# A planned transformer kernel on one core: the division of the exponentials in plain column order, on either of two engines, and a new order of the work

## The chip, the cores and the metric

The kernel runs on one core of a Trainium2 chip. The metric is the device time of one execution in microseconds, the median of the runs. The core has five engines with a queue each: TensorE (PE, with its weight loads PEld), VectorE (DVE), ScalarE (ACT), GpSimd (POOL) and SyncE (SP), which issues most of the transfers here. A queue is worked in order; engines wait for each other by semaphores.

## The reference

There are 32 sequences of 256 tokens with 256 features, all in float32. The output is `x + ffn(cond(x, f))`.

```python
# cond: queries from f, keys and values from x, 16 heads of 16, one extra self column per query
q = (f + b_self) @ Wq + bq;  k = (x + b_prev) @ Wk + bk;  v = x @ Wv + bv
score = concat(mask(q @ k.T * SCALE), sum(q * k_self) * SCALE)
h = (softmax(score) applied to v and v_self) @ Wo + bo
# ffn: two layers of
qkv = shift_token(h) @ wqkv                  # 8 heads of 64
q, k = rotary(l2norm(q) * qs), rotary(l2norm(k) * ks)
h = h + local_attention(q, k, v) @ wo        # windows of 128 that look one window back; softmax
g = layernorm(shift_token(h)) * lg + lb
a, g = split(g @ w1 + b1);  h = h + (a * gelu(g)) @ w2 + b2
```

The change touches the softmax of the local attention: the exponentials of each row are divided by their sum.

## The kernel before

**Groups.** Sixteen groups of two sequences each (`G = 2`) run through the same stages: `prepared` and `conditioned` (the cond layer), `attention` and `feedforward` for each of the two layers, `finished`. Activations of a group lie in one of two kept tiles `stream`, features on the partitions.

**A recorded program and a planner.** The kernel's engine calls do not issue anything. `Plan.record` stores each as a node with a cost (`price`) and its dependences. Everything that PE does between two calls of `plan.unit` is one PE unit, named in the profile by its PSUM tile: `S`, `ST`, `AV` are the cond attention; `q`, `k`, `v`, `qkT`, `sc`, `exT`, `av`, `wout` the local attention; `mean`, `var`, `rs`, `w` the feed-forward; `cq`, `ck`, `cs`, `vals`, `self`, `nmT`, `ohT`, `turn`, `co` the rest of cond. `Plan.run` plays the nodes through a list schedule of its own, with prices for every engine, for hops between engines, for PSUM banks (8) and SBUF slots, and the resulting order is what `Plan.issue` emits (line 567 for every instruction). Which unit PE takes next is chosen by `policy` at the end of `tile_kernel`: the score is the age of a unit (`AGE * u.stand`), a cost for a change of PE's tile mode (`SWITCH`), backlogs of the fed engines (`OVER`, `STAY`, `ENTER`), and `FEED`, `MOST`, `BANKS`. `u.stand` is a place in an ideal order, 215 us per group, shifted unit by unit by the tables `SHIFT`, `FIRST` (first group) and `FINAL` (last two groups). So the tables and the prices set the order of the whole program.

**Tile modes of PE.** A matmul uses the full 128x128 array, or one of the tiled modes: two or four row tiles (`("rows", 2)`: `qkT`, `sc`, `exT`; `("rows", 4)`: `S`, `ST`), two or four column tiles (`("cols", 2)`: `av`; `("cols", 4)`: `AV`). A unit of full matmuls that stands behind one in column tiles can stay in that mode (`tiling`, `parted`): each matmul is then issued in 2 or 4 parts side by side. In the profile `128*64` and `128*32` are the column tiles, `64*128`, `17*128` and `18*128` the row tiles.

**Either engine.** Nodes of engine `X` (`either`) are copies out of PSUM; `put` in `Plan.run` gives each to DVE or ACT, to whichever would end it first by the plan's backlog.

**The softmax of the local attention** (`weights`). For each of two heads (`i`) and two windows (`w`; one or two blocks of 128 keys) DVE adds the mask and takes the row maximum (`ex<-sc,misc`, which frees the PSUM bank of `sc`), ACT takes the exponential with the row sum (`ex<-ex,nm,rq`, `den`), DVE takes the reciprocal of `den` and multiplies the rows by it (`ex<-ex,den`), always on DVE, through a view with the columns in another order: for the wide one `es[:, i, 1:3, :].rearrange("p k q -> p q k")`, so that the inner loop has two elements 128 columns apart. Then PE transposes `ex` (`exT`). There are 1024 of these multiplications, half of 128 columns and half of 256.

**POOL** adds the two parts of the rotated q and k (`raw<-raw,rot`), raises norms to the power -1/2 (`rq`, `ss`), scales k (`raw<-raw,ss`), and does some sums (`at`, `tv`, `sq`, `xs`, `ot`).

Of the kernel before, what the change touches and what calls it, by code (L numbers as in the profile page):

```python
# [22 lines left out]
G = 2  # L23
# [125 lines left out]
class Node:  # L149


    def __init__(self, engine, unit, number):
        self.engine, self.unit, self.number = engine, unit or self, number
        self.ops, self.cost, self.table, self.load = [], 0.0, None, 0.0
        self.after, self.then, self.ready, self.tiles = {}, [], 0.0, set()


class Plan:
# [15 lines left out]
    def __init__(self, tc, engines, pools, make):  # L174
        self.tc, self.engines, self.pools, self.make = tc, engines, pools, make
        self.nodes, self.units, self.unit_, self.group, self.place = [], [], None, 0, 0.0
        self.stage, self.stages, self.done = 0, {}, set()


    def tile(self, pool, name, shape):  # L180
# [52 lines left out]
    def record(self, engine, name, args, kw):  # L233
# [6 lines left out]
        if engine == "PE":  # L240
            node, wide = u, int(np.prod(out.shape[1:]))
            u.soft = u.soft and name == "matmul" and kw["lhsT"].shape[1] == 128
            cost = (2 if name == "transpose" else 4) * (wide + 2) / 2400 / u.streams
            if name == "transpose" and u.streams > 1:
                cost = max(cost, 0.062 / u.streams)
            cost = max(cost, 0.2) if wide < 64 else cost
            u.small += wide < 64
            turn = 0.65 if name == "transpose" else 1.0 if wide >= 64 else 0.0
            u.weight += cost * turn * self.WORK.get(u.kind, 1.0)
            u.place += cost  # L250
            self.place += cost
        else:
            node = self.node(engine, u)
            self.edge(u, node)
            if name == "dma_start":

                dst, src = kw["out"].shape, kw["in_"].shape
                run = min(dst[-1], src[-1])
                cost, node.load = 0.55, int(np.prod(dst)) / run * max(0.048, run * 4 / 24e3) / 16
            else:  # L260
                cost, node.table = self.price(engine, name, args, kw, size)
                if engine == "X":
                    node.either = {"V": cost, "S": 0.068 + size / 1267}
                u.feeds[engine] = u.feeds.get(engine, 0.0) + cost
# [10 lines left out]
    def price(self, engine, name, args, kw, size):  # L275

        if engine in "VX":
            extra = 0.02 if name == "reciprocal" else 0.0
            if name == "scalar_tensor_tensor":
                extra = 0.06  # L280
            return 0.065 + extra + size / 960, "any" if engine == "X" else None
        if engine == "S":
            func = args[2] if name == "activation" else None
            table = "exp" if func is AF.Exp else "gelu" if func is AF.Gelu else "any"
            extra = 0.315 if "accum_out" in kw else 0.11 if table == "gelu" else 0.0
            extra += 0.09 if func is AF.Identity else 0.0
            return 0.068 + size / 1267 + extra, table
        power = any(v is ALU.pow for v in args)
        return (0.35 + 0.158 * size if power else 0.1 + (0.00187 if size <= 256 else 0.00215) * size), None

# [3 lines left out]
    def run(self, policy):  # L294
# [4 lines left out]
        units, self.backlog = [], {e: 0.0 for e in "VSGDX"}  # L299
        left = {n: len(n.after) for n in self.nodes}  # L300
        self.kind, self.table, pe, blocked = ("full", 1), "any", 0.0, 0.0
        self.begin()
        self.tick, self.filled, self.warm = 0, 0.0, False
        for n in self.nodes:
# [3 lines left out]
        for u in self.units:  # L308
            for tiles in u.takes.values():
                for t in tiles:  # L310
                    t.lead = u.cost if t.lead is None else t.lead
                tiles.sort(key=lambda t: t.lead)
        self.idle = self.switches = self.cold = self.wire = 0.0

        def put(n):
            if n.engine == "PE":
# [40 lines left out]
        while todo:  # L357
# [12 lines left out]
            if e != "PE":  # L370
                ready = [n for n in waiting[e] if n.ready <= t]
                n = min(ready, key=lambda n: self.rank(n, e))
                waiting[e].remove(n)
                cost = n.cost
                if e == "S" and n.table not in ("any", None, self.table):
                    self.table, cost = n.table, cost + 1.3
                now[e] = t + cost
# [3 lines left out]
                todo -= 1  # L381
                end = t + cost
                if n.load:
                    self.wire = max(self.wire, end) + n.load
                    end = self.wire + self.LANDING
                ended(n, end)
                continue
            fit = {u: fits(u) for u in units if u.ready <= t}
# [148 lines left out]

    def rank(self, n, e):
        other = e == "S" and n.table not in ("any", None, self.table)
        return n.ready + 2.0 * other, n.number  # L540


    def parted(self, u):
# [8 lines left out]
    def issue(self, order):  # L552
# [7 lines left out]
        for n in order:  # L560
# [3 lines left out]
            for name, args, kw in ops:  # L564
                if n.engine in "VS" and name == "copy":
                    name = "tensor_copy" if n.engine == "V" else "copy"
                ins = getattr(self.engines[n.engine], name)(  # L567
                    *[real(v) for v in args], **{k: real(v) for k, v in kw.items()}
                )
# [3 lines left out]
class Engine:  # L573
# [12 lines left out]


SHIFT = [
    156, 528, 54, -76, 49, 292, -28, 245, 120, -102, -425, 52, -30, 35, 68, 22, 33, 22, -208,
    -4, 119, -41, 61, 69, 90, 152, 19, 32, -62, -238, 52, -2, 49, -168, 13, -85, -54, -65, 36,  # L590
    64, 112, -439, -349, -167, 223, -408, -5, 62, -46, -234, 56, -27, 119, -7, -45, 96, -17,
    -38, 61, -374, -335, -58, 1, -150, -372, -152, -51, -265, -409, 8, 67, -53, 114, -41, -17,
    -83, 34, 68, 48, 60, -261, -99, -7, -76, -335, -100, -105, -191, -306, -58, 15, -102, 32,
    -23, -66, 39, -309, -188, 106, -258, 33, -30, -139, 22, -141, 82, -290, -255, 32, 19, -99,
    134, 126, 14, -15, -222, -574, -156, 97, 93, -32, -241, 50, 152, -118, -41, -45, 21, -102,
    20, 47, 3, 15, 55, 169, -56, -24, 43, 199, -247, 143, -97, -15, -223, -41, -95, -88, -212,
    -127, -29, -32, -285, -545, -142, -265, -8, -118, -6, 152, 84, -122, 25, 14, 4, 18, 141, 60,
    166, -454, -139, 25, -127, -186, -20,
]
FIRST = [  # L600
    0, 0, 0, 0, 0, 0, 0, 0, 10, 35, -9, 213, 102, 95, 210, -345, -65, -122, -290, 49, -201, 6,
    -193, -61, -7, 106, 99, -6, -100, -16, 106, 13, 65, -266, -137, 7, -58, 247, 58, 69, 48, 1,
    -114, -155, -32, -173, -34, 65, 135, 130, -117, 69, 71, 117, 272, 156, 73, -3, -1, -31, -33,
    -133, 51, 151, 175, 239, 445, 215, 231, 120, 135, 97, -3, -90, -188, -357, -32, -64, -276,
    -297, -374, -330, -535, -346, -72, -135, -217, 156, 27, 182, 40, -174, -48, 77, -252, -118,
    -307, -246, 33, -96, -400, -238, -150, -69, -239, 6, 79, 152, 26, -38, -60, -358, -15, -155,
    89, -99, -69, -60, 87, -3, -114, -222, -118, 60, -143, -246, -29, -171, -319, -115, -49,
    -17, -96, -75, -88, 113, 144, -56, -6, 35, -9, -141, -41, -74, -183, -115, -131, -49, -79,
    109, -65, -145, 55, -88, -244, -157, -153, -264, -181, -118, -121, -82, -23, -37, -86, -83,
    -110, -213, -219, -209, -160, -63, 0, 0,  # L610
]
FINAL = [
    0, 0, 0, 0, 0, 0, 0, 0, 56, -34, 24, 16, 12, 140, -55, -63, -14, 1, -33, -84, -66, -53, -46,
    -145, -40, -121, 67, -19, -32, -29, 98, 97, 8, 45, -119, -130, -61, -106, 67, 94, -33, 8,
    54, 33, 8, -94, -222, -47, -210, -95, -90, -11, -121, 156, 49, 10, 43, 87, 7, 64, -144, -81,
    35, -80, 47, -31, -76, -182, 53, 86, 32, 67, 229, 49, 115, 31, 6, -10, -135, 40, 27, -79,
    -83, -8, 108, -110, 63, -40, -249, -98, -95, -18, -170, -139, -28, -12, -41, 76, 83, 116,
    59, -9, 65, -157, -74, -50, -119, -145, -16, -25, 13, 6, 73, -2, -181, -184, -151, -49, -97,
    116, -8, 56, 187, 15, 69, -31, -42, -59, 109, 161, 193, 112, 209, 211, 117, 80, 41, 59, 77,
    -84, 136, 47, 92, -54, 145, 66, 93, 1, -60, 152, -30, 108, 108, -119, 50, -9, -29, -39, 44,  # L620
    -113, -118, -128, -103, 66, 10, -89, -27, -49, -2, -10, 53, 34, -67, -8,
]


# [1 line left out]
def tile_kernel(ctx: ExitStack, tc: tile.TileContext, a: dict, out: bass.AP):  # L626
# [415 lines left out]
    def attention(l, b, res):  # L1042
# [80 lines left out]
        def weights(c, sc):  # L1123
# [29 lines left out]
                        accum_out=den[:, i, w : w + 1],  # L1153
                    )
            vec.reciprocal(den, den)

            for i in range(2):
                for w in range(2):
                    part = (
                        es[:, i, 1:3, :].rearrange("p k q -> p q k")  # L1160
                        if w
                        else es[:, i, 0, :].rearrange("p (k q) -> p q k", k=2)
                    )
                    vec.tensor_scalar(part, part, den[:, i, w : w + 1], None, ALU.mult)
            return es

        def turned(ess):
# [207 lines left out]

    PERIOD = 215.0
    STRETCH, AHEAD, LAST = 2.75, 3, 14
    AGE, SWITCH, OVER, STAY, ENTER = 0.02, 1.5, 1.0, 6.0, 4.0
    HURRY = 0.0
    FEED, MOST, BANKS = 1.0, 3.0, 0.0  # L1380


    numbers = {}
# [68 lines left out]
```

## Time and profile before

| | |
|---|---|
| median of 3 runs | 3427.64 us (3423.55 to 3428.22) |
| the profiled execution | 3422.27 us, of which the span is 3420.5 us |
| mean granted clock of TensorE | 0.990 |
| PE busy | 3348.6 us, 98% of the span |
| DVE, ACT, POOL busy | 2161.9 us (63%), 1780.5 us (52%), 1163.4 us (34%) |
| `ex<-ex,den` on DVE | 1024 instructions, 351.4 us |
| loads of ACT's function table | 96 of 1283 ns |

How to read it: the groups overlap, so PE is occupied from one end to the other except in the first 125 us or so, where loads from memory and a halved clock hold it. From about 800 to 2650 us the groups repeat each other exactly, one every 207.2 us; a stretch of that length is the unit in which a change of the steady part is read. A busy PE can still stand inside a matmul's record, so idle time on PE is only a part of what it loses.

### The profile page before, as it was taken

How to read it: one execution, taken by the hardware profiler on the slowest of the kernel's cores; microseconds unless marked ns; L12 is line 12 of the kernel's file. 1: busy time of each engine (PE TensorE's matmuls, PEld its weight loads, DVE VectorE, ACT ScalarE, POOL GpSimd, SP SyncE). 2: the span in 40 equal slices, each digit the busy share in tenths (PEclk: the TensorE clock that was granted, in tenths of full speed). 3: DMA queues.
4: the chain of work that ended last, by engine and by line, in shares of the span. 5: the costliest groups of instructions: out<-in, count | busy, mean ns of one | idle time of the engine just before them, and what ended most of it. 6: DMA issues, size and time to landing. Idle time of an engine off the chain costs nothing.

```text
span 3420.5 us, 69279 instructions
## 1 busy us (share of the span) xinstructions
PE 3348.6 (98%) x25984; PEld 1908.7 (56%) x25984; DVE 2161.9 (63%) x6673; ACT 1780.5 (52%) x4537; POOL 1163.4 (34%) x1195
## 2 busy tenths in 40 slices
PE   6999999999999999999999999999999999999998
PEld 5665556465564655656455564655646556465554
DVE  3558567485675747657485674847657486574763
ACT  0556456473554726456373563735547364554653
POOL 0325052250613407043160522507134070432541
PEclk7999999999999999999999999999999999999999
DMA  5100010010101001010010100101010010100001
GB/s 147 20 15 11 12 27 9 16 26 9 26 15 21 17 13 20 16 20 17 13 21 14 27 13 15 24 7 26 16 20 17 13 20 15 27 15 12 4 2 27
DMA packets 310926, 69.00 MB, mean 20 GB/s; under 512 B 286776, under 2 KB 308096, under 8 KB 310592
## 3 DMA queue, kind: packets, MB, share of 16 engines
q1 hardware_dynamic: 298848, 54.24, 9.3%
q10 hardware_dynamic: 11744, 10.34, 1.1%
q8 instruction: 207, 3.39, 0.4%
q14 instruction: 127, 1.04, 0.1%
HBM read 35.53 MB, written 8.39 MB: 13 GB/s over the span
## 4 chain that ended last, share of the span: by engine, by line
PE 77%; DVE 12%; POOL 3%; ACT 1%; issue 1%; POOLq 0%; SPq 0%; DMA 0%; DVEq 0%; ACTq 0%
PE w L567 27%; DVE ex L567 6%; PE wout L567 6%; PE q L567 5%; PE av L567 4%; PE k L567 4%; PE sc L567 4%; PE S L567 4%; PE v L567 3%; PE ST L567 3%; PE vals L567 3%; PE AV L567 3%; PE exT L567 2%; PE qkT L567 2%; DVE rot L567 2%; PE cs L567 2%
## 5 line engine op out<-in xcount | busy, mean ns | idle before, releaser
L567 ACT ACTIVATE ex<-ex,nm,rq 128x128 f32<-128x128 f32 (+1 forms) x1024 | 546.2, 537 | 107.3 <-DVE nm L567 106.1
L567 PE MATMUL w<-cen,w 128*128 128x512 f32 (+2 forms) x1480 | 589.2, 598 | 0.8 <-DVE cen L567 0.3
L567 POOL TENSOR_TENSOR raw<-raw,rot 128x512 f32<-128x512 f32 x256 | 327.6, 1281 | 749.2 <-DVE rot L567 660.3
L567 PEld LDWEIGHTS w<-cen,w 128*128 128x128 f32 (+2 forms) x1480 | 224.9, 175 | 270.7 <-issue 231.4
L567 DVE TENSOR_SCALAR ex<-ex,den 128x128 f32<-128x128 f32 (+1 forms) x1024 | 351.4, 457 | 5.2
L567 DVE TENSOR_REDUCE mx<-S 128x2 f32<-128x512 f32 x512 | 314.3, 686 | 49.4 <-PE S L567 49.3
L567 PE MATMUL w<-act,w 128*128 128x512 f32 (+3 forms) x880 | 324.6, 602 | 2.9 <-DVE act L567 2.8
L567 ACT ACTIVATE eT<-ST 128x512 f32<-128x512 f32 x512 | 263.8, 605 | 115.0 <-PE ST L567 109.8
L567 DVE CUSTOM_DVE_ANT_0 ex<-sc,misc 128x128 f32<-128x128 f32 (+1 forms) x1024 | 299.2, 353 | 31.3 <-PE sc L567 30.8
L567 DVE SCALAR_TENSOR_TENSOR act<-w,b,act 128x512 f32<-128x512 f32 (+1 forms) x192 | 143.4, 748 | 262.0 <-PE w L567 195.5
L567 ACT ACTIVATE act<-w,b 128x512 f32<-128x512 f32 (+1 forms) x192 | 128.9, 686 | 280.1 <-PE w L567 276.8
L567 POOL TENSOR_TENSOR xs<-stream 128x512 f32<-128x512 f32 x32 | 35.0, 1094 | 641.5 <-PE cs L567 318.1
L567 PE MATMUL wout<-qT,wout 128*64 128x256 f32 (+2 forms) x1728 | 242.8, 381 | 0.5 <-DVE nm L567 0.3
L567 PE MATMUL v<-wqkv,stream 128*128 128x512 f32 (+1 forms) x608 | 242.5, 599 | 0.0
L567 PE MATMUL k<-wqkv,stream 128*32 128x512 f32 (+2 forms) x1104 | 239.9, 593 | 0.0
L567 PE MATMUL q<-wqkv,stream 128*32 128x512 f32 (+2 forms) x960 | 237.7, 594 | 0.2 <-ACT stream L567 0.2
L567 ACT COPY exT<-exT 128x384 f32<-128x384 f32 x512 | 207.3, 498 | 54.5 <-PE exT L567 53.8
L567 PEld LDWEIGHTS w<-act,w 128*128 128x128 f32 (+3 forms) x880 | 124.8, 176 | 167.1 <-issue 151.5
L567 POOL TENSOR_TENSOR rq<-ss,minus_half 128x8 f32<-128x8 f32 x128 | 215.1, 1684 | 4.9
L567 POOL TENSOR_TENSOR ss<-ss,minus_half 128x8 f32<-128x8 f32 x128 | 213.3, 1666 | 5.7
L567 PE MATMUL sc<-kT,qT 64*128 64x128 f32 (+1 forms) x2048 | 205.7, 337 | 0.4
L567 PEld LDWEIGHTS wout<-qT,wout 128*64 128x64 f32 (+2 forms) x1728 | 161.6, 147 | 73.0 <-issue 17.6
(127 smaller groups left out, 5520.2 us busy)
## 6 DMA issues: line engine op xcount, KB each, us to landing
ft<-in_fside_BxSxS_dram SPq DMA_DIRECT2D x128, 64.0 KB
xt<-in_x_dram SPq DMA_DIRECT2D x128, 64.0 KB
qh<-qc SPq DMA_DIRECT2D x256, 32.0 KB
kh<-kc SPq DMA_DIRECT2D x256, 32.0 KB
ot<-in_x_dram SPq DMA_DIRECT2D x128, 64.0 KB
out_dram<-ot SPq DMA_DIRECT2D x128, 64.0 KB
wqkv<-in_L_ffn_wqkv_dram ACTq DMA_DIRECT2D x2, 1536.0 KB
w<-in_L_ffn_w_dram ACTq DMA_DIRECT2D x2, 1364.0 KB
```

The lines of the kernel that those rows point to most:

```text
L567: ins = getattr(self.engines[n.engine], name)(*[real(v) for v in args], **{k: real(v) for k, v in kw.items()})
```

## The change

It does five things.

1. The division in `weights` goes through the plain view of the columns, and to `either` instead of DVE: a node `scaled` becomes `tensor_scalar` (multiply) on DVE or an `activation` (Copy with a scale per partition) on ACT.
2. The planner learns a hold: a POOL instruction of 64 columns or more (`holds`) keeps DVE instructions that have two operands in SBUF and are `scaled`, `tensor_scalar` or `scalar_tensor_tensor` (`port`) from starting before it is nearly done.
3. Prices: `tensor_scalar` and `scaled` in SBUF cost `0.128 + size / 1920` on DVE; POOL's `tensor_scalar` costs 0.205.
4. In the plan a transfer can be issued only when the eighth before it has landed; `rank` of the waiting nodes takes the stand of their unit into account (`HURRY = 0.001`).
5. `STAY` goes from 6 to 5, `MOST` from 3 to 2, `BANKS` from 0 to 1, and all numbers of `SHIFT`, `FIRST` and `FINAL` are new. With them the order of the whole program is new on every engine. No kernel arithmetic is added or removed apart from the division's engine.

```diff
@@ record
+                inside = [v for v in views if not v.tile.pool == "bank"]
+                two = name in ("scaled", "scalar_tensor_tensor", "tensor_scalar") and size >= 4
+                node.port = engine in "VX" and two and len(inside) == len(views)
+                node.holds = engine == "G" and size >= 64
@@ price
+            if name in ("tensor_scalar", "scaled") and args[0].tile.pool != "bank" and size >= 64:
+                return 0.128 + size / 1920, None
...
+        if name == "tensor_scalar":
+            return 0.205, None
@@ run
+                if n.port and e == "V":
+                    t = max(t, held)
+                elif n.holds:
+                    held = t + cost - 0.12
...
-                    self.wire = max(self.wire, end) + n.load
+                    at = max(t, self.landed[-8]) + cost
+                    now[e] = at
+                    self.wire = max(self.wire, at) + n.load
                     end = self.wire + self.LANDING
+                    self.landed.append(end)
@@ rank
-        return n.ready + 2.0 * other, n.number
+        return n.ready + 2.0 * other + self.hurry * n.unit.stand, n.number
@@ issue
+                if name == "scaled" and n.engine == "V":
+                    name, args = "tensor_scalar", (*args, None, ALU.mult)
+                elif name == "scaled":
+                    name, args, kw = "activation", (*args[:2], AF.Copy), {"scale": args[2]}
@@ SHIFT, FIRST, FINAL: all numbers
...
@@ weights
             for i in range(2):
                 for w in range(2):
-                    part = (
-                        es[:, i, 1:3, :].rearrange("p k q -> p q k")
-                        if w
-                        else es[:, i, 0, :].rearrange("p (k q) -> p q k", k=2)
-                    )
-                    vec.tensor_scalar(part, part, den[:, i, w : w + 1], None, ALU.mult)
+                    either.scaled(flat[i][w], flat[i][w], den[:, i, w : w + 1])
@@ tile_kernel
-    AGE, SWITCH, OVER, STAY, ENTER = 0.02, 1.5, 1.0, 6.0, 4.0
-    HURRY = 0.0
-    FEED, MOST, BANKS = 1.0, 3.0, 0.0
+    AGE, SWITCH, OVER, STAY, ENTER = 0.02, 1.5, 1.0, 5.0, 4.0
+    HURRY = 0.001
+    FEED, MOST, BANKS = 1.0, 2.0, 1.0
```

## The prediction

> **What bounds the kernel now.** I read the page first, then a steady stretch by windows, then the groups by shape, then the timeline of one stretch.
>
> ```profile
> span 3420.5 us, 69279 instructions
> PE 3348.6 (98%) x25984; PEld 1908.7 (56%) x25984; DVE 2161.9 (63%) x6673; ACT 1780.5 (52%) x4537; POOL 1163.4 (34%) x1195
> ...
> PEclk7999999999999999999999999999999999999999
> ```
>
> PE is the bound, and its granted clock is full after the first slice. A change pays only through PE: fewer or cheaper instructions there, or less standing still.
>
> ```profile
> core 0: us, PE busy (x) PEld busy (x) DVE busy (x) ACT busy (x) POOL busy (x), PEclk, DMA share, GB/s
> 1400.10:1607.30 207.20, 205.20 (x1626) 114.57 (x1622) 133.86 (x414) 111.03 (x284) 72.97 (x74) 1.00 0.10 18
> ```
>
> In one steady period of 207.20 us DVE has 73 us to spare and ACT 96. To see what PE loses I took the start-to-start spacing of PE's 2531 units, and for each kind, tile mode and change of mode the lower quartile after 130 us. With these, the 158 units of a period add up to 201.6 us, so 5.6 us of 207.2 are standing still. The same sum over the whole program is 3233 us of the 3401 us between the first and the last matmul; most of the rest lies before 215 us.
>
> ```profile
> PE ck L567 <- DVE nm L567: 0.9, 1, 0.9
> PE exT L567 <- ACT sq L567: 0.5, 1, 0.5
> PE turn L567 <- POOL at L567: 0.2, 1, 0.2
> PE qkT L567 <- DVE rot L567: 0.2, 1, 0.2
> ```
>
> These are PE's named waits in that period, 1.8 us; the others hide inside records. The largest excesses stand at `qkT` before `ck` (1.0 us), `exT` (0.8), `qkT` before `v` (0.7), `sc` before `av` (0.5), `turn` (0.5), `S` before `w` (0.45). Behind the first three stands DVE: a PSUM bank or an `ex` that it gave back late.
>
> **The division on DVE.**
>
> ```profile
> L567 DVE TENSOR_SCALAR ex<-ex,den 128x256 f32<-128x256 f32 x512 | 263.8, 518 | 0.0
> ...
> L567 DVE TENSOR_SCALAR ex<-ex,den 128x128 f32<-128x128 f32 x512 | 203.0, 396 | 5.2
> ...
> L567 DVE COPY qh<-misc 128x2048 f32<-128x2048 f32 x1 | 1.2, 1206 | 0.0
> ...
> L567 DVE TENSOR_SCALAR behind<-iota,lens 32x256 f32<-32x256 f32 x1 | 0.3, 340 | 0.1
> ```
>
> ```profile
> 1523.03 1.16 DVE L567 TENSOR_SCALAR ex<-ex,den 128x128 f32<-128x128 f32 x4
> ...
> 1525.44 1.27 POOL L567 TENSOR_TENSOR raw<-raw,rot 128x512 f32<-128x512 f32 x1 [3.56 <-DVE den L567]
> ...
> 1526.41 2.01 DVE L567 TENSOR_SCALAR ex<-ex,den 128x128 f32<-128x128 f32 x4
> ...
> 1526.66 1.28 POOL L567 TENSOR_TENSOR at<-tv,den 128x256 f32<-128x256 f32 x2
> ```
>
> Four divisions (two narrow, two wide) take 1.16 us alone and 2.01 us where POOL's wide operations run: DVE stands until POOL is through. The second run ends just before the `exT` that loses 0.8 us. In all the 1024 occupy 351.4 us; 256 fours at 1.16 are 297, so some 54 us are this hold.
>
> The two programs' instruction lists say where the divisions go: 714 stay on DVE (348 narrow, 366 wide), 310 go to ACT (164 and 146). A plain-ordered division isn't in the trace. Bounds for four: 1.16 us as now, and from the 340 ns for 256 plain columns (and 0.59 ns a column of the 2048-column copy, so 0.265 for 128) 1.21 us of records, which overlap by about 0.1 each like those of now (0.29 each where the records say 0.33 and 0.47), so 0.8. I take 1.0, nearer the plain rows. 714 are 178.5 fours: 143 to 207 us, 178 taken; hold left over 0 to 38 us (as often per instruction as now), 15 taken. DVE is relieved of 351 - 193 = 158 us, 10 a period.
>
> Here a rule speaks against the first part. The Trainium skill ("VectorE: DVE Perf Modes", "What auto-detection actually checks") gives a one-input operation in SBUF its doubled two-port rate when the outermost dimensions are even or equal, which the old view satisfies too; by it the plain order buys no rate at all and keeps the hold, and DVE's relief would be the 310 that leave plus what the order avoids, some 100 to 145 us.
>
> **ACT.** 310 divisions: 233 ns for 32 columns in SBUF (`es`) and 641 for 512 (`sq<-cen`) put them near 0.31 and 0.41 us, 111 us; the exponentials' own 485 and 588 ns bound them from above (165 us), 0.23 each from below (71). The lists also show 126 table loads for 96: 30 x 1.283 = 38 us. ACT goes from 111 to about 120 us a period: no bound, but `eT` and `exT` wait behind it. The median distance in PE work from `ST` to the `AV` that needs ACT's exponentials shrinks from 3.8 to 2.5 us, against 1.7 us that they usually take.
>
> **PE gets dearer.** The arithmetic is the same, but the lists show 1137 changes of tile mode for 1064, and more small matmuls in full tiles: `var` in 20 units for 6, `self` in 18 for 8.
>
> ```profile
> L567 PE MATMUL self<-misc,prod 128*64 128x8 f32 x368 | 13.8, 201 | 0.0
> L567 PE MATMUL var<-mean_w,sq 128*64 128x1 f32 x368 | 13.4, 194 | 0.0
> ...
> L567 PE MATMUL self<-misc,prod 128*128 128x8 f32 x64 | 9.0, 264 | 2.4 <-DVE prod L567 2.4
> L567 PE MATMUL var<-mean_w,sq 128*128 128x1 f32 x48 | 6.0, 246 | 0.0
> ```
>
> A unit of `var` costs 13.4 / 23 = 0.58 us in column tiles and 6.0 / 6 = 1.0 in the full array, `self` 0.60 and 1.12: 14 x 0.42 + 10 x 0.52 = 11 us more.
>
> ```profile
> 1436.07 1.98 PE L567 MATMUL w<-cen,w1t 128*128 128x512 f32 x4
> 1437.89 3.60 PE L567 MATMUL w<-cen,w 128*128 128x512 f32 x8
> 1441.42 2.09 PE L567 MATMUL S<-kh,qh 17*128 17x256 f32 x32
> ```
>
> The first unit behind `S` takes 1.82 us to the next start, two more and the way out 3.53, where a unit in the midst takes 1.72: about 0.1 us to enter and 0.1 to leave. By the quartiles a change costs 0.1 to 0.2 us; 73 more are 7 to 15, 10 taken. Sum: 21 us; pricing every unit of the new list gives 3257 for 3233, 24 us, and 203.6 for 201.6 in a steady period. I take 22 (18 to 26).
>
> **The stalls.** What can come back is at most the 5.6 us of a period. The three places behind DVE are 2.5 us. In the new order the distances there are longer: a bank of `sc` is wanted again no sooner than 1.0 us (2nd percentile; 0 before), one of `q` 3.2 us (2.1 before; DVE and ACT need 2.2 to release it), and from `sc` to `exT` there are 10.3 us at the 10th percentile (8.8 before) for a chain made shorter. Others shrink: a bank of `k` 1.8 (3.0 before, 2.2 needed), `k` to `qkT` 8.0 (8.9), `at` to `turn` 2.0 (4.3, 2.8 needed). What is late next is POOL's chain to `qkT` and `turn`. I take 2.5 us a period over 14 periods, 35 us (0 to 78). The first 215 us keep their loads and their slow clock; the new list sets the second layer's `b` units ahead of the first `S`, which wait for the last weights, but has more of the second sequence's work ahead of them; -15 to +15, 0 taken. SP's transfers are the same in number, and PE is not waiting for SP in the steady part.
>
> **Sum.** +22 - 35 + 0 = -13 us on 3422.27, 3409.3. The median of the runs stands 5.4 us above the profiled execution, which I carry over: 3414.6, said as 3414.
>
> **The rivals.**
>
> *Slower: the extra work on PE isn't repaid.* It is there for certain, 22 us; if less than 22 / 14 = 1.6 us of stall goes in a period, the kernel loses. For it: PE is 98% busy, the named waits are 1.8 us a period, and some distances got shorter. Against: the hold stands right before a loss. With stalls unchanged 3449.
>
> *No change that can be measured* (within 0.2%, about what a measurement of this kernel can tell from no change, 7 us): the plain order does nothing, the hold hits as often per instruction, and 1.6 us a period go through the order alone: 3427.
>
> *A larger gain:* all 5.6 us of a period go: 78 - 22 = 56, 3371. Against it stand `turn` behind POOL and `ck`, `AV` behind a busier ACT.
>
> **How the numbers follow.** The forecast (3395 to 3420) has 0.45, the larger gain 0.10, no change 0.14, slower 0.31. Faster 0.55, same 0.14, slower 0.31. The range 3380 to 3452 leaves out the lower part of the larger gain and a loss beyond unchanged stalls; the forecast's own range is 3395 to 3420.
>
> **What would show it.** Right: a steady period of about 206.5 us, DVE near 124 and ACT near 120 us in it, the four divisions near 1.0 us and rarely above 1.3, the named waits for DVE gone from PE's list, PE's units worth 203.6. Wrong: a period of 208 or more with waits for ACT or POOL in their place, or divisions that still stand behind POOL.

## The result: slower by 0.4%, and the profile after

| | before | after |
|---|---|---|
| median of the runs | 3426.37 us (7 runs, 3422.09 to 3429.11) | 3438.13 us (7 runs, 3435.71 to 3442.12) |
| ratio, 95% interval | | 1.0039, 1.0030 to 1.0049 |
| span of the profiled execution | 3420.5 us | 3436.4 us |
| a steady period | 207.2 us | 208.8 us |

The kernel became about 12 us slower. The forecast was 3414 us; the time lies inside the range, but on the side of the rival "the extra work on PE isn't repaid". The head of the changed kernel's page, engines first and then the granted clock by slices:

```profile
span 3436.4 us, 67247 instructions
PE 3382.7 (98%) x25120; PEld 1962.1 (57%) x25120; DVE 2072.9 (60%) x6383; ACT 1917.5 (56%) x4857; POOL 1168.4 (34%) x1195
...
PEclk8999999999999999999999999999999999999999
```

PE is still busy 98% of the span, with 864 matmuls fewer and 34 us more of busy time. DVE lost 89 us, ACT gained 137. The clock is the same, so the time is not lost there. The same view of a steady period as before the change, with the same columns (span of the stretch, then busy time and number of instructions of PE, PEld, DVE, ACT and POOL, the clock, the share of the DMA engines and GB/s):

```profile
1431.84:1640.59 208.75, 208.01 (x1581) 119.40 (x1580) 129.51 (x399) 119.23 (x302) 72.84 (x74) 1.00 0.10 18
```

DVE has 129.5 us for 133.9, ACT 119.2 for 111.0, and the period is 1.6 us longer. PE's named waits in this stretch (total, times, longest):

```profile
PE v L591 <- ACT v L591: 0.4, 1, 0.4
PE sc L591 <- DVE stream L591: 0.2, 1, 0.2
```

They were 1.8 us before and are 0.6 now. Anyone who read only this list would expect a gain. But the list never held more than a part of what PE stands still, as busy records can contain standing too, so it took a run of PE alone to see the rest.

The divisions, by shape on each engine (number of instructions, then busy time and the mean duration in ns, then idle time before them), with the loads of ACT's table:

```profile
L591 DVE TENSOR_SCALAR ex<-ex,den 128x256 f32<-128x256 f32 x366 | 135.7, 375 | 0.1
L591 DVE TENSOR_SCALAR ex<-ex,den 128x128 f32<-128x128 f32 x348 | 133.5, 384 | 3.9
```

```profile
L591 ACT ACTIVATE ex<-ex,den 128x256 f32<-128x256 f32 x146 | 72.6, 499 | 0.5 <-DVE den L591 0.5
L591 ACT ACTIVATE ex<-ex,den 128x128 f32<-128x128 f32 x164 | 64.9, 397 | 11.7 <-DVE den L591 9.6 <-DVE rstd L591 0.6
L591 ACT ACT_TABLE_LOAD x126 | 161.7, 1283 | 51.8 <-DMA b<-in_L_ffn_b_dram 33.2 <-PE w L591 11.6 <-PE ST L591 5.0
```

The narrow divisions on DVE have a longer mean than the wide ones. That can't be their work; it is the hold. The view of the tile shows it (shortest, median and longest duration), and so does the timeline (start, duration, engine):

```profile
L591 DVE TENSOR_SCALAR ex<-ex,den x714: 271/342/1375, 187.0 to 3357.8; 128x256 f32<-128x256 f32 x93, 128x128 f32<-128x128 f32 x86
```

```profile
1564.32 1.27 POOL L591 TENSOR_TENSOR raw<-raw,rot 128x512 f32<-128x512 f32 x1
1564.59 1.83 DVE L591 TENSOR_SCALAR ex<-ex,den 128x128 f32<-128x128 f32 x4
...
1578.70 1.01 DVE L591 TENSOR_SCALAR ex<-ex,den 128x128 f32<-128x128 f32 x4
```

Four divisions take 1.01 us where POOL is not in a wide operation and 1.83 us where they start beside one. The free durations (medians of the divisions that no POOL instruction overlaps) are 281 ns (narrow) and 347 ns (wide), which makes the hold about 46 us in 714 instructions, 64 ns each; before they were 326 and 473 ns, and the hold was about 60 us in 1024, 58 ns each. Of the 161 fours that run without a gap in the new kernel 62 take more than 1.3 us, of the old kernel's 256 there are 61.

PE's small matmuls by shape (`128*128` is the full array):

```profile
L591 PE MATMUL var<-mean_w,sq 128*128 128x1 f32 x160 | 20.3, 248 | 0.0
L591 PE MATMUL self<-misc,prod 128*128 128x8 f32 x144 | 18.3, 254 | 0.0
L591 PE MATMUL self<-misc,prod 128*64 128x8 f32 x224 | 8.2, 199 | 0.0
L591 PE MATMUL var<-mean_w,sq 128*64 128x1 f32 x176 | 6.5, 194 | 0.7 <-DVE mx L591 0.7
```

The 20 units of `var` and 18 of `self` in the full array are there as the instruction list said, at 1.02 us each, where a unit in two column tiles takes 0.59.

### The profile page after: what moved, and what is told of

It is laid out like the page before. It is cut to its first block, busy times and chain, and to the rows that moved or that the text cites. A ratio compares the mean times of both kernels' runs of the same rounds, so it can differ in the third digit from the quotient of the medians.

```text
span 3436.4 us, 67247 instructions
## 1 busy us (share of the span) xinstructions
PE 3382.7 (98%) x25120; PEld 1962.1 (57%) x25120; DVE 2072.9 (60%) x6383; ACT 1917.5 (56%) x4857; POOL 1168.4 (34%) x1195
## 4 chain that ended last, share of the span: by engine, by line
PE 82%; DVE 10%; ACT 6%; DMA 1%; issue 1%; POOL 0%; DVEq 0%; ACTq 0%; SPq 0%; POOLq 0%
PE w L591 27%; PE q L591 6%; PE wout L591 5%; PE k L591 5%; PE av L591 5%; PE ST L591 4%; PE v L591 4%; ACT ex L591 4%; DVE ex L591 4%; PE AV L591 4%; PE S L591 4%; PE sc L591 4%; PE vals L591 3%; PE exT L591 2%; PE ck L591 2%; PE cs L591 2%
## 5 line engine op out<-in xcount | busy, mean ns | idle before, releaser
L591 PE MATMUL w<-cen,w 128*128 128x512 f32 (+2 forms) x1400 | 580.9, 598 | 0.2 <-DVE cen L591 0.2
L591 PEld LDWEIGHTS w<-cen,w 128*128 128x128 f32 (+2 forms) x1400 | 234.5, 181 | 274.9 <-issue 249.5
L591 PE MATMUL k<-wqkv,stream 128*32 128x512 f32 (+2 forms) x992 | 251.2, 595 | 0.0
L591 PE MATMUL q<-wqkv,stream 128*128 128x512 f32 (+2 forms) x748 | 241.6, 599 | 0.3 <-ACT stream L591 0.2
L591 PE MATMUL wout<-qT,wout 128*64 128x256 f32 (+1 forms) x1792 | 234.8, 380 | 0.1
L591 DVE TENSOR_SCALAR ex<-ex,den 128x256 f32<-128x256 f32 (+1 forms) x714 | 227.1, 379 | 4.0
L591 PEld LDWEIGHTS wout<-qT,wout 128*64 128x64 f32 (+1 forms) x1792 | 156.9, 144 | 77.8 <-issue 10.6
```

Source lines behind the costliest of these rows:

```text
L591: ins = getattr(self.engines[n.engine], name)(*[real(v) for v in args], **{k: real(v) for k, v in kw.items()})
```

## The experiments

**The theories.** *Extra work*: PE's own work in the new order is some 22 to 24 us dearer, and the change gave back less standing still than that. *The orders cost PE alike*: the priced difference is an artefact of pricing by quartiles, and the new order stands still more. A second pair concerns the division: *it costs what I credited* (2.5 us a period), or *it costs little in the steady part* and a lighter DVE has little to give there. In what follows a period is the time from one group's first `mean` to the next group's, and the nine in the middle are the steady ones.

### PE's matmuls alone, in the old and in the new order

All matmuls in the order of the kernel, with everything else left out but the output transfers and one load; the operands are set once, and each PSUM bank is given back by a copy of one column.

```diff
@@ issue (the same in both kernels)
+ only nodes of PE are issued; every SBUF tile is set once by memset 0.5
+ behind the last PE unit of a PSUM tile: a copy of one column, on DVE and ACT in turn
```

> The old order of PE's matmuls with nothing else in it: every SBUF tile is set once, all other work is left out, and each PSUM bank is given back by a read of one column. Own-work theory (the new order costs TensorE more work, and what it stands still for is the same in both): a steady period of 201.6 us, the sum of the shortest usual spacings, so 5.6 us of the 207.2 us are standing still. Rival (the 5.6 us are no standing still but work that the sum misses): about 207 us here too.

> The same for the new order. Own-work theory: a steady period of 203.6 us, 2.0 us above the old order alone, and over the whole program some 24 us more than it. Rival (new waits: the new order is slower because ScalarE, with 310 divisions and 30 more table loads, or GpSimd is late): the two orders alone differ by less than 0.5 us a period, and the difference of the full kernels comes from the other engines.

Measured: 3322.74 us (ratio to the kernel before 0.9704, 0.9685 to 0.9724) with the old order, 3348.42 us (0.9779, 0.9757 to 0.9801) with the new one. Steady stretches of the old and of the new order, columns as above:

```profile
1382.99:1585.65 202.66, 202.66 (x1644) 113.95 (x1642) 20.39 (x129) 20.53 (x129) 0.00 (x0) 1.00 0.00 1
```

```profile
1400.60:1605.10 204.50, 204.50 (x1581) 116.72 (x1580) 20.43 (x129) 20.64 (x129) 0.00 (x0) 1.00 0.00 1
```

The new order costs PE 25.7 us more with nobody to wait for, 1.8 us a period; the prices had said 24 and 2.0. Each has two runs, and they lie 22 to 29 us apart. The theory that the orders cost alike falls. These stretches also give the standing still: 207.2 - 202.7 = 4.5 us a period before, 208.8 - 204.5 = 4.3 after. The quartiles had 201.6 and 203.6 us for PE's own work, 1.1 and 0.9 too few, and so 5.6 us of standing still before. In the whole program the kernel lost 12 us for 25.7 of extra work, so some 14 us of standing still did go, most of it outside the nine steady periods (9 x 0.2 = 2, or 3 by the means of the nine).

### The division left out, in the old and in the new kernel

```diff
@@ issue
+                if n is a division: continue
```

> The old order, with the 1024 divisions not issued (the weights stay undivided). Own-work theory: VectorE is relieved of 351 us and holds against GpSimd are gone, yet TensorE loses only what stands behind the divisions, at most 1 us a period: 3410 to 3426 us. The forecast's step (2.5 us a period stand behind VectorE): 40 us less, near 3387 us.

> The new order, with the divisions not issued. Own-work theory: 3420 to 3437 us, still at or above the old order without divisions by 10 to 25 us. Rival (new waits behind the divisions on ScalarE and the hold on VectorE): it falls to 3415 us or less, to the level of the old order without divisions.

Measured: 3388.3 us (0.9896, 0.9879 to 0.9913) and 3410.51 us (0.9958, 0.9942 to 0.9975). Steady stretches of the old and of the new kernel without the division:

```profile
1408.68:1614.60 205.92, 204.95 (x1644) 114.94 (x1642) 115.45 (x350) 111.27 (x284) 72.11 (x74) 1.00 0.10 18
```

```profile
1418.55:1625.15 206.60, 206.60 (x1582) 118.86 (x1580) 115.32 (x352) 113.69 (x285) 72.62 (x74) 1.00 0.10 18
```

This is the run that decides. With every division gone and the order kept, a steady period of the old kernel falls only from 207.3 to 205.9 us (means of the nine). All that hangs on the division there is 1.3 us a period, 12 us over the nine steady ones, though DVE is 18 us less busy. In total 36 us hang on the divisions, close to the 35 that I had counted; but 8.5 of these lie in the first three groups and 15 in the last three, where fewer groups overlap. In the new kernel the division costs 26 to 28 us in total, and in a steady period 1.9 us: more than before, although DVE does 30% fewer of them. It costs less than before at the ends, 6 us in the first three groups and 2 in the last three.

Neither expectation holds whole. The old kernel's total is the forecast's 3387, and its steady period is close to the "at most 1 us" of the other theory. The new kernel fell to the rival's 3415 or less, but not to the old order's level without divisions: 22 us stay between them.

The order of PE's units is the same with and without the division and in the run of PE alone, so their starts can be compared place by place. By how many us a steady period PE's next start comes later than in the run of PE alone:

| place | with the division | without |
|---|---|---|
| old order, `qkT` before `ck` | 0.24 in eight periods, 1.01 in one | 0.24 |
| old order, `exT` before `q` | 0.76 | 0.80 |
| old order, `qkT` before `v` | 0.76 | 0.00 |
| new order, `sc` before `av` | 0.75 | 0.00 |
| new order, `exT` before `sc` | 0.74 | 0.00 |
| new order, `exT` before `v` | 0.47 | 0.00 |

The first three are the places on which the forecast counted. Only `qkT` before `v` stood behind the division; the 1.0 us at `ck` belongs to the one period that was read; and `exT` waits as before, for ACT. PE's list for the whole program has, in the old kernel and without the division:

```profile
PE exT L567 <- ACT sq L567: 5.5, 11, 0.5
PE exT L569 <- ACT sq L569: 5.8, 11, 0.5
```

In the new order nothing is lost behind `qkT` any more, and the three other places of the table have come, all three behind the division.

So the account of the change is: 26 us of extra PE work, 8 us less for the division, 4 to 5 us less for other waits (what is left of the 21 to 22 us between the two kernels without division, against 25.7), together 13 us slower. With two to four runs of each program, a part is good to some 3 us.

### The division's plain view alone

```diff
@@ weights, in the old kernel and its order
-                    vec.tensor_scalar(part, part, den[:, i, w : w + 1], None, ALU.mult)
+                    vec.tensor_scalar(flat[i][w], flat[i][w], den[:, i, w : w + 1], None, ALU.mult)
```

> The old kernel with one edit: the division goes through the plain view of the columns, still always on VectorE; the order on every engine is the old one. Own-work theory: a plain division is issued on 0.195 and 0.262 us after the one before in the new kernel, a permuted one on 0.18 and 0.29, and it stands behind GpSimd all the same, so 3421 to 3428 us, no change. Rival (plain order is worth what the forecast said, 0.16 us for four): VectorE's divisions fall from 351 to below 300 us and the time by 5 us or more.

Measured: 3417.90 us, 0.9987 (0.9977 to 0.9996) in 11 runs. The divisions of this kernel by shape:

```profile
L567 DVE TENSOR_SCALAR ex<-ex,den 128x256 f32<-128x256 f32 x512 | 199.3, 389 | 0.0
L567 DVE TENSOR_SCALAR ex<-ex,den 128x128 f32<-128x128 f32 x512 | 175.4, 343 | 4.9
```

They occupy 311.3 us in place of 351.4, and the gain is 0.13%: a little faster than the 3421 to 3428 us of the one theory, and with more on DVE than the 300 us of the other. The records are shorter, but the spacing of divisions that follow each other hardly changes: behind another division 0.196 and 0.263 us (128 and 256 columns) for 0.180 and 0.292; the first of a four takes 0.20 in both. That is 0.92 us for four instead of 0.97. As many divisions as before still stand beside POOL's wide operations, its sums and products of 256 or 512 columns (98 narrow and 47 wide; 99 and 49 before).

### The divisions that were held, moved to ACT

89 divisions that stood behind POOL in the old kernel are issued on ACT, at their places in the old order.

```diff
@@ issue, in the old kernel
+                if n is a division and its number is in HELD:
+                    n.engine, ops = "S", [("activation", (out_, in_, AF.Copy), {"scale": den})]
```

> The old order with the old view; the 89 divisions that ran over 0.12 us longer than usual in the old profile (they stood behind GpSimd) are issued on ScalarE instead, at the same place of the program. Without any division the old order took 36 us less. If what the divisions cost is the hold, these 89 carry most of it: 3395 to 3412 us, which would beat both kernels. If it is the length of the chain through VectorE, 3418 to 3426 us.

Measured: 3430.41 us, 1.0024 (1.0012 to 1.0035): slower, which neither theory had expected. A steady stretch, PE's waits in it, and the divisions left on DVE:

```profile
1417.27:1625.47 208.20, 205.57 (x1645) 115.04 (x1643) 133.72 (x409) 113.33 (x289) 73.30 (x74) 1.00 0.10 18
```

```profile
PE exT L579 <- ACT sq L579: 1.7, 1, 1.7
PE ck L579 <- DVE nm L579: 0.6, 1, 0.6
PE turn L579 <- POOL at L579: 0.3, 1, 0.3
```

```profile
L579 DVE TENSOR_SCALAR ex<-ex,den 128x256 f32<-128x256 f32 x482 | 269.4, 564 | 1.1
```

Five divisions of a period leave DVE and the period grows by 1.0 us. First, a queue in a fixed order passes the delay on: `exT`, which waits for ACT, now waits 1.7 us for 0.5. That is more than the 0.76 us at `qkT` before `v`, which did go. Second, the hold is not a property of these divisions: the mean of the wide ones that stayed rose from 518 to 564 ns, and 74 of them stood beside POOL instead of 49. Fewer narrow ones did (40 for 99), yet the hold of all that stayed is as large as that of all before (about 63 us for 60). At the end of the program it helped all the same: the last of the group intervals fell from 201.8 to 197.3 us, though the one before it grew from 240.1 to 243.3. This is why a later kernel moves divisions at the ends alone.

### All divisions back on DVE, in the new order

```diff
@@ issue, in the new kernel
+                if n.ops and n.ops[0][0] == "scaled": n.engine = "V"
```

> The new order, with the 310 divisions of ScalarE issued on VectorE at the same place of the program, plain view. Own-work theory with the order fitted to its prices: VectorE takes some 75 to 100 us more and more of it stands behind GpSimd; 3440 to 3460 us. Rival (ScalarE's divisions made the new order slow): 3437 us or less.

Measured: 3456.51 us, 1.0102 (1.0086 to 1.0118), 18 to 21 us slower than the changed kernel (by the medians, and by the ratios to the kernel before). But its steady period is 208.3 us (mean of the nine), no worse than the 208.8 with ACT's share; the loss lies at the ends, 10 us of it in the first interval between groups (187.8 us for 177.9). A list of PE's waits in the whole program has this:

```profile
PE exT L593 <- DVE ex L593: 5.2, 10, 0.9
PE exT L593 <- ACT sq L593: 4.9, 10, 0.7
```

All ten waits of the first row stand at the two ends, nine of the second row's ten in the steady part. With the divisions back on DVE `sc` before `av` loses 0.13 us for 0.75 and `exT` before `v` nothing for 0.47, while `exT` before `sc` loses 1.06 for 0.74. So ACT's share of the divisions is worth some 20 us to this order, and none of it is in the steady part, for which I had credited it.

### `var` and `self` in the full array, in the old order

```diff
@@ issue, in the old kernel
+                if n.engine == "PE" and n.ops and n.small and n.soft: n.tiling = ("full", 1)
```

> The old order; the 50 units of var and self that stood in column tiles are issued in the full array, which also makes 66 more changes of tile mode. By the prices of the forecast (0.42 and 0.52 us a unit, 0.1 to 0.2 us a change) TensorE has 33 us more work: 3447 to 3457 us if it shows in full, less where the longer units fall into time in which it stood still. Rival (small matmuls and changes are hidden in time that TensorE stands still anyway): below 3435 us.

Measured: 3455.27 us, 1.0093 (1.0077 to 1.0108), 31.5 us for 50 more units in the full array and 66 more changes of tile mode, which the prices of the prediction put at 33.

```profile
L569 PE MATMUL self<-misc,prod 128*128 128x8 f32 x256 | 34.1, 259 | 1.4 <-DVE prod L569 1.4
L569 PE MATMUL var<-mean_w,sq 128*128 128x1 f32 x256 | 33.4, 251 | 0.1
```

Such a unit takes 1.07 and 1.04 us here. So PE's extra work, as priced, reaches the end of the program nearly whole; PE has no slack here in which a cheap-looking change of its order could hide.

### The old order with plain view and ACT at the ends

From the runs so far: keep the old order, take the plain view, and move only held divisions of the first 560 us and the last 250 us (26 of them) to ACT. A second version moves one division in each middle group as well.

```diff
@@ issue, in the old kernel with the plain view
+                if n is a division and its number is in ENDS:        # the second version: ENDS and one per middle group
+                    n.engine, ops = "S", [("activation", (out_, in_, AF.Copy), {"scale": den})]
```

> The old order with the plain view, and of the 89 divisions that stood behind GpSimd only the 26 of the first 560 us and the last 250 us issued on ScalarE. By the periods of the two runs before (all 89 moved against plain alone: -0.5 and -2.4 us in the first two groups, -5.8 us in the last, but +1.2 us in each steady one) 3409 to 3416 us, which would beat both kernels. Rival (the losses of the steady groups come with any division on ScalarE): 3419 us or more.

> The same, and in each of the eleven groups between one division more on ScalarE: the one that stood 0.9 us behind GpSimd ahead of the wait of 0.6 us between qkT and v. If that wait is the hold's, it goes: some 6 us less than the run with the ends alone, 3403 to 3410 us. Rival (ScalarE's queue gives it back): no less than the ends alone.

Measured: 3410.22 us, 0.9959 (0.9945 to 0.9972) for the ends alone, 3412.96 us, 0.9971 (0.9959 to 0.9982) with the middle ones. The first beats the kernel before by 14 us, as expected, and the changed one by some 27.

```profile
1417.38:1624.33 206.95, 205.87 (x1645) 115.30 (x1643) 132.64 (x414) 111.16 (x284) 72.11 (x74) 1.00 0.10 18
```

Its steady period is that of the plain view (207.0 us), and the last group interval is 196.4 us for 201.8. With one division of each middle group on ACT the period is 207.4: in the middle ACT gives it back, as its rival had it. The wait between `qkT` and `v` for which that division was moved does go, 0.58 us a period, but `exT` before `q` loses 1.65 us for 0.77, and in PE's waits for the whole program the 5.5 us above have become

```profile
PE exT L576 <- ACT sq L576: 15.2, 11, 1.4
```

The difference between the two totals (3 us) is within their intervals.

### The new planner with the old tables

```diff
@@ the new kernel
+ SHIFT, FIRST, FINAL, STAY, MOST, BANKS, HURRY of the old kernel
```

> The new kernel with the old tables SHIFT, FIRST and FINAL and the old STAY, MOST, BANKS and HURRY, so the new planner's prices and the division on either engine, but an order that nobody fitted to them. Its list prices TensorE's own work at 3255 us, 22 us above the old order. Own-work theory: at least 3440 us, and more if the order stands still more often. Rival (the parts other than the new numbers bring the loss or the gain by themselves): within 10 us of one of the two kernels.

Measured: 3522.12 us, 1.0288 (1.0269 to 1.0307). The prices put PE's own work in this order at 3255 us, about that of the changed kernel (3257), so most of the 84 us between them should be standing still; a run of PE alone in this order was not made, and the mean granted clock is lower too (0.979 for 0.990), which accounts for a part that no run separates. The tables fit the plan for which they were found, and the edits to the planner can't be judged without finding new ones. Which of the settings (`STAY`, `MOST`, `BANKS` or the tables) made PE's work dearer stays open for the same reason.

## Why the prediction was wrong, step by step

**The step that failed is the -35 us of "the stalls": 2.5 us a period over 14 periods.** Its parts:
- *The size of the cover.* I took the excess at three places behind DVE (2.5 us) as what a lighter DVE would give back. With no division at all, 1.3 us come back, 0.76 of it at one of the three places, `qkT` before `v`. The 1.0 us at `ck` was one period's; the others have 0.24, which stay. At `exT` nothing comes back: the list of waits that I showed names ACT there, not DVE, and the held divisions that end just before it were not its cause. An excess beside a busy engine is not a wait for the work that this engine will lose.
- *The 14 periods.* The 36 us that hang on the division, of which I had the total nearly right by luck, are 12 us in nine steady periods and 23 at the ends. Multiplying a steady period by 14 gave the right total from the wrong place, and the changed kernel's relief in the steady part bought nothing.
- *What is late next.* I named POOL's chain to `qkT` and `turn`. By the same start-to-start spacings the steady stretch now loses 0.7 us at `exT` before `sc` and `sc` before `av` each, 0.6 at `S` before `w` and `ST` before `AV`, 0.5 at `exT` before `v`: many small places, with hardly a named wait among them. Three of them, 1.9 us together, go with the division, so late next was the division itself, in places that the new order made tight. Standing still went from 4.5 to 4.3 us a period, where I had 5.6 to 3.1.

**+22 us of PE work: right.** 25.7 us measured (22 to 29 by single runs), inside the 18 to 26 given, near the 24 of pricing every unit. The parts are confirmed for the small matmuls (1.02 us a unit); the 73 changes of tile mode were not measured by themselves. The Trainium skill ("TensorEngine Tiling (Array Packing)", "Key Properties") says that a change of tiling mode drains the engine; it gives no figure, and the 25.7 us contain it.

**DVE's relief: 158 taken, 124 measured** (351.4 to 227.1 us). Four divisions at 1.0 us were right (1.01). The hold was not: 15 us taken, 46 measured. The plan knows POOL's hold and the list was ordered by it, yet per instruction the hold grew from 58 to 64 ns; no run shows why the planned order missed it on the chip. DVE as a whole lost only 89 us, 4.3 in a steady period where 10 were taken: 17 of a period's 64 divisions left it, not 19, and 20 more copies in the whole program and longer records of `nm<-nm,rq` (55.9 us for 49.1) took some of the relief back. The rule of the Trainium skill quoted in the prediction ("VectorE: DVE Perf Modes", "What auto-detection actually checks") was closer in what it implied, 100 to 145 us, partly by luck: the plain view alone takes 40 us off the records of 1024 divisions (351.4 to 311.3), which the rule put at nothing, and a larger hold hides it. In its detail the runs differ from it: from 128 to 256 columns the spacing grows by 0.88 ns a column in the permuted view and by 0.52 ns in the plain one, so an added column costs the plain view little more than half as much, while both stand behind POOL. By these two widths the permuted view has the smaller fixed part, which makes up for most of it.

**ACT: right in the period, low in the price.** 119.2 us a period for "about 120"; but a division takes 397 and 499 ns where 310 and 410 were taken, 137.5 us for 111. The upper bounds (485 and 588) held. That a steady period has 17 divisions on ACT and not the 19 of an even share offsets part of the low price.

**The ramp: 0 taken, within -15 to +15.** The first `mean` of the first group comes 4 us earlier (210.4 for 214.5), which is no clear change, as this point lies between 206 and 219 us in the profiles of the old order's runs. The first three group intervals take 10 us longer; PE's own work in them, by the runs of PE alone, grew by nearly 12.

**The rival.** "If less than 1.6 us of stall goes in a period the kernel loses" is what happened: 0.2 to 0.3 went. Its 3449 for unchanged stalls lies 11 us above the time: the extra work was 4 us dearer, and some 14 us of standing still went, nearly all of it outside the steady periods.

## What to carry to other kernels

Where one engine is busy from end to end, price its own instructions in the new order first, and check that price by running it alone; here this part reached the end nearly whole. What relief on another engine gives back is not read from excesses that stand beside it: leave that work out at a fixed order and see how far the steady period falls, and the ends by themselves. Read such an excess from several periods, not from one. In this kernel moving work to an idle engine paid where few stages run at once, at the start and the end; in the steady part an in-order queue passed five moved instructions on as a microsecond of new waiting.

## What the runs showed of the chip

- A division on DVE that starts beside a wide operation of POOL ends only with it (up to 1320 ns for 281 in 128 columns, 1375 for 347 in 256). In the new kernel all 75 that start with more than 300 ns of such an operation to go end 0.08 to 0.15 us behind its end; the 72 that start with as much to go of one of POOL's powers (`minus_half`, 4 or 8 columns, 1.0 to 1.9 us) take 276 to 349 ns, as free ones do. Moving the ones that were held does not remove the hold; others take their places (49 wide ones before, 74 after).
- Behind another division, the same multiplication of 128 columns starts the next one sooner in the permuted view (0.180 us) than in the plain one (0.196), and the other way round for 256 (0.292 and 0.263).
- In the old order DVE, ACT and POOL work 134, 111 and 73 us in a steady period, and all that they and the transfers add to PE's time is 4.5 us of 207.2; the other 202.7 are what PE takes alone.
